# First sequences fetched by register, softmax by halves, first rows asked for per expert, in a fused two-layer mixture-of-experts and attention kernel

## Chip, cores and metric

The kernel runs on one core of a Trainium2 chip, in float32. A core has five engines that work side by side, each through its own queue in order: TensorE (PE, matrix products and transposes), VectorE (DVE), ScalarE (ACT), GpSimd (POOL) and SyncE (SP, which issues DMAs). ACT and POOL issue DMAs too. The metric is the device time of one execution in microseconds, as a median of several.

## Reference

Inputs are `x` (32 sequences of 64 rows of 256), gate probabilities of 32 sequences for 8 experts, a shared gate probability and a label `itok` per sequence, drawn from 0 to 2.

```
# first layer: dense mixture, then attention, added to x
c = (1 - sg) * sum_e prob[b,e] * (silu(x@Wg[e]) * (x@Wu[e])) @ Wd[e]  +  sg * shared(x)
q,k,v = c@W_qkv + b_qkv                       # 16 heads of 16
score = -arccosh(<q,k> on the hyperboloid)**2 / 4, causal
x = x + (softmax(score) * spike @ v) @ W_out + b_out

# second layer: an expert chosen by the label, two shared ones, weighed by a small gate
eo = relu(x@wi[label])@wo[label];  s0, s1 = relu(x@swi[i])@swo[i]
w  = softmax(relu([eo[:,0], s0[:,0], s1[:,0]] @ g1) @ g2)    # first row of each sequence
d  = eo*w0 + s0*w1 + s1*w2
d  = d + causal_attention(conv(layernorm(d)))                # rotary, softmax
d  = d + top1_moe(layernorm(d))                              # 4 experts
out = x + d
```

## The kernel before, in words

**Order of the sequences.** `order_of_sequences` (L127 to L220) reads the 32 labels twice, once as a row on every partition (`lab_row`) and once as a column (`lab_col`), both from ACT's queue, and sorts the sequences by label with small steps on DVE and three tiny matmuls: `row`, `col`, `same`, `lower`, ranks, `place`, and the one-hot `at` (L185). Two matmuls (L188, L189) turn `at` into row addresses of x (`tokens`, L193; as integers `tokens_i`, L196) and the sorted labels (`label`, L197). A constant block `setup`, also loaded by ACT, holds index tables used in these steps (at L158, L186, L193).

**Taking x in.** `gather` (L222 to L231) fetches 128 rows with an indirect DMA that POOL issues, at addresses from `tokens_i`. Rows come by blocks of 512 (eight sequences, four gathers). `take_in` (L558 to L569) transposes a block on PE (L565), copies it to `xT` (L566, two copies on DVE) and forms its sums `xS` (L537 to L541). The gathers of blocks 1 to 3 are asked for during the first expert.

**The dense mixture, L736 to about 1330 us.** Nine experts (the ninth is the shared one) over four blocks of 512 rows, each product cut into Strassen-like parts. `xg` (L777, POOL) is x weighed by the gate, `right` makes its sums `gS`, `left` (L492 to L500, DVE) the sums `wsum` of weights. `up` (L639) gives the up products: matmuls at L653, copies out of PSUM by ACT (L665), sums by DVE (L673), silu by ACT (L674). `down` (L599) is the down product. Weights come over SP, with one exception: the third of all, the first expert's Wd, goes out on POOL behind the first block's gathers (`issue_after(first_in)`). Beside the ninth expert's last blocks runs the first attention group, `hyperbolic(0)`.

**The middle, 1330 to 2110 us.** Eight groups of two tiles of 128 rows. A group passes through hyperbolic attention, `selected` (L883: two shared relu experts through `dense`, L899 and L913, then the chosen experts, L951 to L977; for some groups each half tile has its own weights, fetched at the label read into a register), `gated_sum` (L996), `rotary` and `route`. The steps of several groups are woven. For the first six groups, `selected` collects the first rows of all three outputs `eo[0..2]` in a tile `firsts` with six little DMAs (L993), and `gated_sum` transposes them at L1015.

**Attention.** `attend` (L335 to L387) works on scores `s` of 128 rows by 16 heads x 64 columns, `za` in the hyperbolic layer. Softmax is three whole steps: the maximum by heads (L339, DVE), the subtraction (L340, POOL), the exponential (L341, ACT). Then PE transposes in two lots of four (L348), copied out by DVE and ACT (L350, L352), and multiplies by the values `vb` (L359). Before it, scores are made at L307 (L264 to L296 prepare them) and masked at L331.

**The tail** is the mixture of four experts by blocks of sorted rows (L1408 to L1475).

**What sets the order.** Engines work their queues in order. A list scheduler fills the queues from the program's order, its own costs of instructions, and hints `issue_after(x)`, which keep an instruction behind x in that order. A tile in a pool with several buffers waits for its buffer's last readers. Completions of DMAs are counted on eight lanes; a DMA's issue waits until the DMA before it on the same lane is complete.

Of the kernel before, what the change touches and what calls it, by code (L numbers as in the profile page):

```python
# [10 lines left out]
F32 = mybir.dt.float32  # L11
I32 = mybir.dt.int32
AF = mybir.ActivationFunctionType
ALU = mybir.AluOpType
AX = mybir.AxisListType
PSUM = bass.MemoryType.PSUM

P = 128
B, S, D, H, HD, F = 32, 64, 256, 16, 16, 1024
NT = B * S // P  # L20
NE, NE2, NE3 = 8, 5, 4
FC = F // P
EPS = 1e-05
# [53 lines left out]
def adaln_attn_ffn_kernel(ctx: ExitStack, tc: tile.TileContext, a, consts, out):  # L77
    nc = tc.nc
    ctx.enter_context(nc.allow_non_contiguous_dma(reason="small per-channel vectors"))
    x_rows = a["x"].flatten_outer_dims()  # L80
    out_rows = out.flatten_outer_dims()

    const = ctx.enter_context(tc.tile_pool(name="const", bufs=1))


    ident = const.tile([P, P], F32, name="ident")
# [3 lines left out]
    tokens = const.tile([P, NT], F32, name="tokens")  # L90
    tokens_i = const.tile([P, NT], I32, name="tokens_i")
    label = const.tile([1, B], I32, name="label")
    causal = cst[:, C_CAUSAL : C_CAUSAL + S]
    headsel = cst[:, C_HEAD : C_HEAD + 4]
    cos = cst[:, C_COS : C_COS + HD]
# [7 lines left out]
    def rows(pool, name, n):  # L103

        t = pool.tile([P, n], F32, name=f"{name}_rows")
        nc.scalar.dma_start(t, a[name].partition_broadcast(P))
        return t

    def channels(name):

        t = const.tile([P, 2], F32, name=f"{name}_chan")
        nc.scalar.dma_start(t, a[name].rearrange("(c p) -> p c", p=P))
        return t
# [3 lines left out]
    def weight(pool, name, src, eng=None):  # L117

        t = pool.tile([P, src.shape[0] // P, src.shape[1]], F32, name=name)
        loaded.append((eng or nc.sync).dma_start(t, src.rearrange("(c p) n -> p c n", p=P)).ins)  # L120
        return t
# [5 lines left out]
    def order_of_sequences(pool, wide, psum, mixw):  # L127
# [4 lines left out]

        small = lambda name, n=1: pool.tile([B, n], F32, name=name)
        lab_row = pool.tile([B, B], I32, name="lab_row")
        nc.scalar.dma_start(lab_row, a["itok_B_0_2"].partition_broadcast(B))
        lab_col = pool.tile([B, 1], I32, name="lab_col")
        nc.scalar.dma_start(lab_col, a["itok_B_0_2"].unsqueeze(1))
        setup = pool.tile([P, C_COLS - C_SETUP], F32, name="setup")
        nc.scalar.dma_start(setup, consts[:, C_SETUP:])
        weights = small("weights", NE + 1)  # L140
# [6 lines left out]
        nc.gpsimd.memset(every, 1.0)  # L147

        row, col = small("row_f", B), small("col_f")
        nc.vector.tensor_scalar(col, lab_col, 0, NE2 - 1, ALU.max, ALU.min)  # L150
        nc.vector.tensor_scalar(row, lab_row, 0, NE2 - 1, ALU.max, ALU.min)
        same, lower = small("same", B), small("lower", B)
        nc.vector.tensor_scalar(same, row, col, None, ALU.is_equal)
        nc.vector.tensor_scalar(lower, row, col, None, ALU.is_gt)

# [29 lines left out]
        nc.vector.tensor_scalar(at, seq, place, None, ALU.is_equal)  # L185
        nc.vector.tensor_scalar(own, every, part, None, ALU.mult)  # L186
        pq = psum.tile([P, 512], F32, name="W1")
        nc.tensor.matmul(pq[:, 0:B], lhsT=own, rhs=at, start=True, stop=True)  # L188
        nc.tensor.matmul(pq[0:1, B : 2 * B], lhsT=col, rhs=at, start=True, stop=True)  # L189
        whose = pq[:, 0:B].rearrange("p (t k) -> p t k", k=2)  # L190
        for k in range(2):
# [1 line left out]
            nc.vector.tensor_scalar(  # L193
                tokens[half], whose[half, :, k], float(S), setup[half, C_POS : C_POS + 1], ALU.mult, ALU.add
            )
        ordered = nc.vector.tensor_copy(tokens_i, tokens).ins  # L196
        nc.vector.tensor_copy(label, pq[0:1, B : 2 * B])  # L197


        with tc.issue_after(ordered):  # L200
# [16 lines left out]
            stop=True,  # L217
# [107 lines left out]
    def heads(t):  # L325
        return t.rearrange("p (h j) -> p h j", j=S)
# [8 lines left out]
    def attend(s, vb, w_out, spike=None):  # L335


        mx = sb.tile([P, H], F32, name="mx", bufs=two)
        nc.vector.tensor_reduce(mx, heads(s), AX.X, ALU.max)  # L339
        nc.gpsimd.tensor_tensor(heads(s), heads(s), mx.unsqueeze(2).to_broadcast([P, H, S]), ALU.subtract)  # L340
        nc.scalar.activation(s, s, AF.Exp)  # L341
        yield
        sT = sb.tile([P, 8, P], F32, name="sT", bufs=two)
        for half in range(2):
            pt = turned()
            for i in range(4):
                hp = 4 * half + i
                nc.tensor.transpose(pt[:, i, :], s[:, hp * P : (hp + 1) * P], ident)  # L348
            if half:
                nc.scalar.copy(sT[:, 4 * half : 4 * half + 4, :], pt)  # L350
            else:
                nc.vector.tensor_copy(sT[:, 4 * half : 4 * half + 4, :], pt)  # L352
            yield
        py = bank([P, H, 17])
        for b2 in range(2):
            for hp in range(8):

                pair = hp % 4 // 2 * 4 + hp // 4 * 2 + hp % 2
                nc.tensor.matmul(  # L359
                    py[b2 * S : (b2 + 1) * S, 2 * pair : 2 * pair + 2, :],  # L360
                    lhsT=sT[:, hp, b2 * S : (b2 + 1) * S],
                    rhs=vb[:, b2, :, pair, :],
                    start=True,
                    stop=True,
                )
        inv = sb.tile([P, H], F32, name="inv", bufs=two)
        nc.vector.reciprocal(inv, py[:, :, 16])
        if spike is not None:
            nc.vector.tensor_scalar(inv, inv, spike, None, ALU.mult)
        y = sb.tile([P, D], F32, name="y", bufs=two)  # L370
        nc.vector.tensor_tensor(
            y.rearrange("p (h d) -> p h d", d=HD),
            py[:, :, 0:HD],
            inv.unsqueeze(2).to_broadcast([P, H, HD]),
            ALU.mult,
        )
        yield
        pt = turned()
        for c in range(2):
            nc.tensor.transpose(pt[:, c, :], y[:, c * P : (c + 1) * P], ident)  # L380
        yT = sb.tile([P, 2, P], F32, name="yT", bufs=two)
        nc.scalar.copy(yT, pt[:, 0:2, :])
        yield
        po = bank([P, D])
        for c in range(2):
            nc.tensor.matmul(po, lhsT=yT[:, c, :], rhs=w_out[:, c, :], start=c == 0, stop=c == 1)
        return po  # L387
# [114 lines left out]
    with ExitStack() as st:  # L502
# [13 lines left out]
        ordered = order_of_sequences(  # L516
            rp, lambda: work.tile([P, 2, TH], F32, name="cp", bufs=10).rearrange("p k n -> p (k n)"), psw, mixw
        )
        b_sur = rows(const, "L0_attn_b_sur", 1)
        threshold = rows(const, "L0_attn_threshold", 1)  # L520
        ln1_w, ln1_b = channels("L0_ffn_ln1_w"), channels("L0_ffn_ln1_b")
        ln2_w, ln2_b = channels("L0_ffn_ln2_w"), channels("L0_ffn_ln2_b")
        conv_w = const.tile([P, 2, 3], F32, name="conv_w")
        nc.scalar.dma_start(conv_w, a["L0_ffn_conv_w"].rearrange("(c p) o k -> p c (o k)", p=P))
        minus_b_sur = const.tile([P, 1], F32, name="minus_b_sur")
        with tc.issue_after(ordered):
            nc.vector.tensor_scalar(minus_b_sur, b_sur, -1.0, None, ALU.mult)
        eps = const.tile([P, 1], F32, name="eps")
        nc.vector.memset(eps, EPS)

        in_sums = None

        def right(eng, b, t):
# [19 lines left out]
        def gather_block(tb):  # L553
            for t in range(4 * tb, 4 * tb + 4, 2):
                got = gather(staged[t // 8][:, t % 8 : t % 8 + 2, :], t)
            return got
# [11 lines left out]
                )  # L568
            x_right.append(right(nc.vector if tb == 0 else nc.gpsimd, xT[tb], xS[tb]))  # L569

        first_in = gather_block(0)
        take_in(0)

        blank = rp.tile([P, ROW], F32, name="blank")
# [146 lines left out]
        for e in range(NE + 1):  # L721
            pick = lambda n, s: a[f"L0_cond_W{n}"][e] if e < NE else a[f"L0_cond_S{s}"]

            def take(left, src):
                nonlocal n_w
                i, j = n_w % 5, n_w % 4
                n_w += 1
                eng = nc.gpsimd if n_w == 3 else nc.sync
                with tc.issue_after(first_in) if n_w == 3 else nullcontext():
                    w = weight(rp if i in (2, 3) else wp, f"w{i}", src, eng)  # L730
                return left(w, (rp if j == 3 else wp).tile([P, 3, Q * P], F32, name=f"wsum{j}"))


# [5 lines left out]
            if e == 1:  # L739

                w_qkv = condp.tile([P, 2, 3 * D + 1], F32, name="w_qkv")
                nc.sync.dma_start(
                    w_qkv[:, :, 0 : 3 * D], a["L0_attn_W_qkv"].rearrange("(c p) n -> p c n", p=P)
                )
                nc.scalar.dma_start(
                    w_qkv[:, :, 3 * D], a["L0_attn_w_sur"].rearrange("(c p) -> p c", p=P)
                )
                b_qkv = rows(condp, "L0_attn_b_qkv", 3 * D)
            if e == 3:

                with tc.issue_after(loaded[-1]):
# [131 lines left out]
    def selected(g, xT):  # L883

        eo = [None] * 3
        output = lambda: rt.tile([P, NG, D], F32, name="eo", bufs=4)

        def dense(w):  # L890
# [32 lines left out]
        for s in range(2):  # L923
            po = yield from dense(slots(a["L0_cond2_swi"][s], a["L0_cond2_swo"][s]))
            eo[1 + s] = output()
            nc.vector.tensor_copy(eo[1 + s], po)

        def chosen(place):
            lab = nc.sync.value_load(label[0:1, place : place + 1], min_val=0, max_val=NE2 - 1)
# [56 lines left out]

        if g >= DIRECT:
            return eo, None

        firsts = hidden([P, 2, GN])[0 : 6 * NG, 0, :]  # L990
        for i in range(3):
            for b2 in range(2):
                nc.scalar.dma_start(firsts[4 * i + b2 : 4 * i + 4 : 2, :], eo[i][b2 * S : b2 * S + 1, :, :])  # L993
        return eo, firsts

    def gated_sum(g, eo, firsts):  # L996
# [567 lines left out]
```

## Time and profile before

| | us |
|---|---|
| median of 3 runs | 2293.69 |
| range of the runs | 2288.44 to 2294.05 |
| profiled execution | 2294.86 |
| its span | 2293.1 |
| mean granted TensorE clock | 0.993 |
| PE idle in the span | 72.1 |
| of it before 50 us | 17.5 |

The span is what the trace covers; the profiled execution's own time has 1.8 us around it. In a line of the page or of the list of groups, an operation has its line in the kernel (L665), engine, output and input tiles, count, busy time, mean duration and the idle time of its engine just before. In the list of waits, `PE X L653 <- ACT cp L665: 3.0, 3, 2.5` says that PE's matmuls into X at L653 stood idle for 3.0 us in 3 places, the longest 2.5, until ACT's copies at L665 ended. In the timeline a line is start, duration, engine, line and form, with the wait before it in brackets. In the table of stretches each row has its length, busy time and count of PE, PEld (weight load), DVE, ACT and POOL, then the granted clock, the DMA share and GB/s.

### The profile page before, as it was taken

The page shows a single profiled execution, that of the slowest core. Times are in us where ns is not written, and L with a number is a line of the kernel's source. Part 1 is how long each engine was busy: PE and PEld are TensorE (multiplying, and loading weights), DVE is VectorE, ACT ScalarE, POOL GpSimd, SP SyncE. Part 2 cuts the span into 40 slices and gives each one's busy share as a digit, 9 for nine tenths or more (in the row PEclk, how much of TensorE's full clock was granted, in tenths as well). Part 3 has the DMA queues.
Part 4 walks back from the last instruction along what each step waited for, and adds up shares of the span by engine and source line. Part 5 has one row for each costly group of instructions (what it writes and reads, how often), then busy time and mean ns, then how long its engine had stood idle before and what let it go on. Part 6 is the DMA issues. An engine that isn't in the chain of part 4 may idle for free. (4 is left out here: it accounts for less than half of the span.)

```text
span 2293.1 us, 29566 instructions
## 1 busy us (share of the span) xinstructions
PE 2221.0 (97%) x11222; PEld 1797.9 (78%) x11222; DVE 1323.4 (58%) x2443; ACT 741.1 (32%) x1184; POOL 799.5 (35%) x665
## 2 busy tenths in 40 slices
PE   6999999999999999999999999999999999989998
PEld 5888888888888888888888776677677677766665
DVE  7466575565655646556565744757757757554222
ACT  2333333333333333333333623424334334222111
POOL 6653444444444544445445350122122111111110
PEclk9999999999999999999999999999999999999999
DMA  3110010190101001001000046233332322540110
GB/s 118 35 37 19 1 38 19 56 309 1 37 19 37 19 1 37 19 18 38 1 19 10 3 142 200 83 121 106 97 94 83 93 87 80 189 136 24 40 38 24
DMA packets 100157, 145.02 MB, mean 63 GB/s; under 512 B 10214, under 2 KB 62000, under 8 KB 100016
## 3 DMA queue, kind: packets, MB, share of 16 engines
q1 hardware_dynamic: 81120, 124.45, 16.7%
q0 software_dynamic: 3952, 11.57, 1.5%
q10 hardware_dynamic: 14944, 7.11, 1.3%
q8 instruction: 90, 1.47, 0.3%
q14 instruction: 51, 0.42, 0.1%
HBM read 114.54 MB, written 24.29 MB: 61 GB/s over the span
## 5 line engine op out<-in xcount | busy, mean ns | idle before, releaser
L665 ACT COPY cp<-X 128x512 f32<-128x512 f32 x432 | 251.1, 585 | 537.2 <-PE X L653 523.7
L673 DVE TENSOR_TENSOR cp<-W,cp 128x512 f32<-128x512 f32 x272 | 186.2, 690 | 84.6 <-ACT cp L665 70.2
L706 POOL TENSOR_TENSOR h_t<-h_t,h_b 128x512 f32<-128x512 f32 x72 | 95.9, 1331 | 355.5 <-DVE h_t L675 355.4
L674 ACT ACTIVATE cp<-cp 128x512 f32<-128x512 f32 x216 | 136.4, 631 | 227.6 <-DVE cp L673 227.6
L777 POOL TENSOR_TENSOR xg<-xT,mixw 128x1024 f32<-128x1024 f32 x36 | 71.2, 1977 | 312.9 <-PE W L653 310.4
L899 PE MATMUL ph<-xT,slot 128*128 128x256 f32 x672 | 167.6, 391 | 1.6 <-ACT h L848 1.5
L913 PE MATMUL ph<-slot,h 128*128 128x256 f32 x672 | 165.1, 386 | 1.4 <-DVE h L850 0.9
L673 DVE TENSOR_TENSOR cp<-Y,cp 128x512 f32<-128x512 f32 x160 | 109.8, 689 | 89.5 <-PE Y L653 77.0
L675 DVE TENSOR_TENSOR h_b<-cp 128x512 f32<-128x512 f32 x144 | 141.3, 981 | 17.6 <-ACT cp L674 1.6
L653 PE MATMUL X<-xS,w 128*128 128x256 f32 x576 | 148.2, 380 | 2.7 <-ACT cp L665 2.7
L653 PE MATMUL X<-gS,w 128*128 128x256 f32 x576 | 148.3, 380 | 0.3 <-ACT cp L665 0.3
L899 PEld LDWEIGHTS ph<-xT,slot 128*128 128x128 f32 x672 | 124.3, 194 | 23.2 <-issue 6.6
L913 PEld LDWEIGHTS ph<-slot,h 128*128 128x128 f32 x672 | 121.8, 190 | 21.3 <-DVE h L850 5.0
L627 DVE TENSOR_TENSOR condT<-downA,condT 128x256 f32<-128x256 f32 x132 | 55.3, 419 | 142.4 <-PE downA L616 142.3
L616 PE MATMUL downA<-h_t,w 128*128 128x256 f32 x576 | 136.3, 379 | 0.0
L653 PEld LDWEIGHTS X<-xS,w 128*128 128x128 f32 x576 | 109.1, 190 | 18.1 <-ACT cp L665 3.8
L653 PEld LDWEIGHTS X<-gS,w 128*128 128x128 f32 x576 | 109.4, 190 | 16.0 <-ACT cp L665 0.7
L616 PEld LDWEIGHTS downA<-h_t,w 128*128 128x128 f32 x576 | 109.6, 190 | 14.7
L627 DVE TENSOR_TENSOR condT<-downB,condT 128x256 f32<-128x256 f32 x104 | 43.4, 417 | 122.9 <-PE downB L616 122.9
L709 POOL TENSOR_TENSOR h_t<-h_b,h_t 128x512 f32<-128x512 f32 x72 | 110.3, 1532 | 0.0
L707 POOL TENSOR_TENSOR h_t<-h_b,h_t 128x512 f32<-128x512 f32 x72 | 104.9, 1456 | 4.2
L708 POOL TENSOR_TENSOR h_t<-h_b,h_t 128x512 f32<-128x512 f32 x72 | 97.0, 1348 | 0.0
(366 smaller groups left out, 4565.1 us busy)
## 6 DMA issues: line engine op xcount, KB each, us to landing
rows_d<-blank SPq DMA_DIRECT2D x67, 258.0 KB
slot<-in_L_cond_swi SPq DMA_DIRECT2D x32, 512.0 KB
slot<-in_L_cond_swo SPq DMA_DIRECT2D x32, 512.0 KB
slot<-in_L_cond_wi SPq DMA_DIRECT2D x26, 512.0 KB
slot<-in_L_cond_wo SPq DMA_DIRECT2D x26, 512.0 KB
w<-in_L_cond_Wg SPq DMA_DIRECT2D x8, 1024.0 KB
w<-in_L_cond_Wu SPq DMA_DIRECT2D x8, 1024.0 KB
w_up<-in_L_ffn_expert_wv SPq DMA_DIRECT2D x16, 512.0 KB
```

The source lines that it names most:

```text
L616: nc.tensor.matmul(po, lhsT=wd[l](q), rhs=h[q // 2][r][:, q % 2, :], start=fresh and q == 0, stop=q == Q - 1, skip_group_check=True,)
L627: nc.vector.tensor_tensor(acc, po, acc, ALU.add)
L653: nc.tensor.matmul(bank[m, name][:, k, :], lhsT=w[l][:, q * P : (q + 1) * P], rhs=src[r], start=fresh and k == 0, stop=True, skip_group_ch ...
L665: nc.scalar.copy(side[m, name], bank[m, "X"])
L673: nc.vector.tensor_tensor(t, bank[m, b], t, ALU.add)
L674: nc.scalar.activation(side["g", name], side["g", name], AF.Silu)
L675: nc.vector.tensor_tensor(h[key], side["g", name], side["u", name], ALU.mult)
L707: nc.gpsimd.tensor_tensor(h["t2"], h["b22"], h["t1"], ALU.subtract)
L708: nc.gpsimd.tensor_tensor(h["t3"], h["b22"], b12, ALU.subtract)
L709: nc.gpsimd.tensor_tensor(h["t4"], h["b21"], h["t2"], ALU.subtract)
L899: nc.tensor.matmul(ph[:, k, :], lhsT=w[half][:, c, fc * P : (fc + 1) * P], rhs=xT[:, c, :], start=c == 0, stop=c == 1,)
L913: nc.tensor.matmul(po[:, k, :], lhsT=hs[fc // 2][:, fc % 2, k * P : (k + 1) * P], rhs=w[2 + fc // 4][:, fc % 4, :], start=fc == 0, stop=fc ...
```

## The change

It has three parts.

1. `lab_col` is gone; `lab_row` goes out on SP; `col` is made from `row` by a product with the identity and a sum. A third small matmul makes `seqs`, the numbers of the first eight sequences in sorted order. SP and ACT read them into registers, four each, and fetch one sequence of 64 rows each at a register address, in place of block 0's four gathers on POOL. A number of small loads on ACT (b_sur to conv_w) and, on SP, the first Wd and w_qkv stand behind these; Wd goes over SP as the other weights do. `minus_b_sur` moves to POOL in the second expert.
2. In `attend`, maximum, subtraction and exponential are done on halves of 512 columns, eight heads each.
3. `firsts` is allotted at the start of `selected`, and the two DMAs of an expert are asked for right behind that expert's output.

```diff
-        nc.scalar.dma_start(lab_row, a["itok_B_0_2"].partition_broadcast(B))
-        lab_col = pool.tile([B, 1], I32, name="lab_col")
-        nc.scalar.dma_start(lab_col, a["itok_B_0_2"].unsqueeze(1))
+        nc.sync.dma_start(lab_row, a["itok_B_0_2"].partition_broadcast(B))
...
         row, col = small("row_f", B), small("col_f")
-        nc.vector.tensor_scalar(col, lab_col, 0, NE2 - 1, ALU.max, ALU.min)
         nc.vector.tensor_scalar(row, lab_row, 0, NE2 - 1, ALU.max, ALU.min)
         same, lower = small("same", B), small("lower", B)
+        nc.vector.tensor_tensor(lower, row, ident[0:B, 0:B], ALU.mult)
+        nc.vector.tensor_reduce(col, lower, AX.X, ALU.add)
...
         pq = psum.tile([P, 512], F32, name="W1")
+        nc.tensor.matmul(pq[0:1, 2 * B : 2 * B + 8], lhsT=part, rhs=at[:, 0:8], start=True, stop=True)
+        first_eight = nc.vector.tensor_copy(seqs, pq[0:1, 2 * B : 2 * B + 8]).ins
...
-        ordered = nc.vector.tensor_copy(tokens_i, tokens).ins
-        nc.vector.tensor_copy(label, pq[0:1, B : 2 * B])
+        with tc.issue_after(first_eight):
+            ordered = nc.vector.tensor_copy(tokens_i, tokens).ins
+            nc.vector.tensor_copy(label, pq[0:1, B : 2 * B])
...
-        nc.vector.tensor_reduce(mx, heads(s), AX.X, ALU.max)
-        nc.gpsimd.tensor_tensor(heads(s), heads(s), mx.unsqueeze(2).to_broadcast([P, H, S]), ALU.subtract)
-        nc.scalar.activation(s, s, AF.Exp)
+        for half in range(2):
+            of = slice(half * 512, (half + 1) * 512)
+            mh = mx[:, half * 8 : half * 8 + 8]
+            nc.vector.tensor_reduce(mh, heads(s[:, of]), AX.X, ALU.max)
+            nc.gpsimd.tensor_tensor(heads(s[:, of]), heads(s[:, of]), mh.unsqueeze(2).to_broadcast([P, 8, S]), ALU.subtract)
+            nc.scalar.activation(s[:, of], s[:, of], AF.Exp)
...
-        first_in = gather_block(0)
+        behind_x = [None, None]
+        for place in range(8):
+            eng = (nc.sync, nc.scalar)[place % 2]
+            seq = eng.value_load(seqs[0:1, place : place + 1], min_val=0, max_val=B - 1)
+            half = place % 2 * S
+            got = eng.dma_start(staged[0][half : half + S, place // 2, :], x_rows[bass.ds(seq * S, S), :])
+            behind_x[place % 2] = got.ins
+        with tc.issue_after(behind_x[1]):
+            b_sur = rows(const, "L0_attn_b_sur", 1)
+            threshold = rows(const, "L0_attn_threshold", 1)
...
-                eng = nc.gpsimd if n_w == 3 else nc.sync
-                with tc.issue_after(first_in) if n_w == 3 else nullcontext():
-                    w = weight(rp if i in (2, 3) else wp, f"w{i}", src, eng)
+                with tc.issue_after(behind_x[0]) if n_w == 3 else nullcontext():
+                    w = weight(rp if i in (2, 3) else wp, f"w{i}", src)
...
+                with tc.issue_after(behind_x[0]), tc.issue_after(behind_x[1]):
+                    nc.sync.dma_start(
+                        w_qkv[:, :, 0 : 3 * D], a["L0_attn_W_qkv"].rearrange("(c p) n -> p c n", p=P)
+                    )
+                    nc.scalar.dma_start(
+                        w_qkv[:, :, 3 * D], a["L0_attn_w_sur"].rearrange("(c p) -> p c", p=P)
+                    )
+                    b_qkv = rows(condp, "L0_attn_b_qkv", 3 * D)
...
+        firsts = hidden([P, 2, GN])[0 : 6 * NG, 0, :] if g < DIRECT else None
+
+        def gather_first(i):
+            for b2 in range(2 if g < DIRECT else 0):
+                nc.scalar.dma_start(firsts[4 * i + b2 : 4 * i + 4 : 2, :], eo[i][b2 * S : b2 * S + 1, :, :])
...
             nc.vector.tensor_copy(eo[1 + s], po)
+            gather_first(1 + s)
...
-        firsts = hidden([P, 2, GN])[0 : 6 * NG, 0, :]
-        for i in range(3):
-            for b2 in range(2):
-                nc.scalar.dma_start(firsts[4 * i + b2 : 4 * i + 4 : 2, :], eo[i][b2 * S : b2 * S + 1, :, :])
+        gather_first(0)
         return eo, firsts
```

More of the change, by code (lines that the diff above doesn't have):

```diff
@@ L92, in adaln_attn_ffn_kernel @@
     label = const.tile([1, B], I32, name="label")
+    seqs = const.tile([1, 8], I32, name="seqs")
     causal = cst[:, C_CAUSAL : C_CAUSAL + S]
@@ L518, in adaln_attn_ffn_kernel @@
         )
[L519 to L529, printed above, removed]
         in_sums = None
@@ L569, in take_in @@
             x_right.append(right(nc.vector if tb == 0 else nc.gpsimd, xT[tb], xS[tb]))
-        first_in = gather_block(0)
+        behind_x = [None, None]
[8 more added lines that the diff above has]
+            threshold = rows(const, "L0_attn_threshold", 1)
+            ln1_w, ln1_b = channels("L0_ffn_ln1_w"), channels("L0_ffn_ln1_b")
+            ln2_w, ln2_b = channels("L0_ffn_ln2_w"), channels("L0_ffn_ln2_b")
+            conv_w = const.tile([P, 2, 3], F32, name="conv_w")
+            nc.scalar.dma_start(conv_w, a["L0_ffn_conv_w"].rearrange("(c p) o k -> p c (o k)", p=P))
+            eps = const.tile([P, 1], F32, name="eps")
+            nc.vector.memset(eps, EPS)
         take_in(0)
@@ L741, in adaln_attn_ffn_kernel @@
                 w_qkv = condp.tile([P, 2, 3 * D + 1], F32, name="w_qkv")
[L742 to L748, printed above, removed]
+                with tc.issue_after(behind_x[0]), tc.issue_after(behind_x[1]):
[6 more added lines that the diff above has]
+                    b_qkv = rows(condp, "L0_attn_b_qkv", 3 * D)
+                minus_b_sur = const.tile([P, 1], F32, name="minus_b_sur")
+                with tc.issue_after(in_sums):
+                    nc.gpsimd.tensor_scalar(minus_b_sur, b_sur, -1.0, None, ALU.mult)
             if e == 3:
```

## The prediction

> **What bounds the kernel now.** I read the totals of the page first, then the busy time by stretches, then TensorE's list of waits, then the timeline of the front and of one softmax, and last how the instructions are ordered after the change.
>
> ```profile
> PE 2221.0 (97%) x11222; PEld 1797.9 (78%) x11222; DVE 1323.4 (58%) x2443; ACT 741.1 (32%) x1184; POOL 799.5 (35%) x665
> ```
>
> TensorE (PE) is busy 2221.0 of 2293.1 us, and the granted clock is 0.993. The change leaves its matmuls as they are (one tiny one is added), so at most the 72.1 us of idle can be won. By stretches (busy us of each engine):
>
> ```profile
> 0.00:10.00 10.00, 0.37 (x4) 0.28 (x4) 3.25 (x23) 0.00 (x0) 1.32 (x9) 1.00 0.75 232
> 10.00:20.00 10.00, 3.94 (x11) 1.93 (x11) 6.17 (x19) 1.28 (x1) 6.21 (x5) 1.00 0.56 165
> 50.00:1200.00 1150.00, 1150.00 (x5337) 1014.31 (x5337) 678.08 (x955) 373.22 (x634) 547.23 (x437) 1.00 0.11 38
> 1400.00:2100.00 700.00, 662.69 (x4118) 488.64 (x4117) 438.12 (x1085) 238.94 (x357) 124.75 (x104) 0.98 0.35 109
> ```
>
> From 50 to 1200 there is no idle to win. 15.7 us lie before 20 us (10 − 0.37 and 10 − 3.94), 37.3 us between 1400 and 2100. The change acts in these two places. The waits of PE by operand and releaser (us, times, longest):
>
> ```profile
> PE W L172 <- DVE kind L169: 8.5, 1, 8.5
> PE ph L1015 <- DMA vb<-v: 5.5, 3, 1.9
> PE pt L348 <- ACT s L341: 5.2, 8, 1.4
> PE ph L1015 <- DMA h<-eo: 4.7, 3, 1.8
> PE X L565 <- DMA w<-in_x,tokens_i: 3.1, 4, 1.6
> PE X L653 <- ACT cp L665: 3.0, 3, 2.5
> PE pt L348 <- ACT za L341: 0.8, 2, 0.5
> ```
>
> The first and fifth are the front, the third and last the softmax (6.0 together), the second and fourth the first rows (10.2 together). Idle on DVE, ACT or POOL counts only where it ends one of these.
>
> **Part 1: the first eight sequences, fetched by register.** The front's chain, in the timeline (start, duration, in brackets the wait):
>
> ```profile
> 4.05 0.17 DVE L151 TENSOR_SCALAR row_f<-lab_row 32x32 f32<-32x32 int32 x1 [3.18 <-DMA lab_row<-in_itok_B]
> 6.17 0.14 DVE L150 TENSOR_SCALAR col_f<-lab_col 32x1 f32<-32x1 int32 x1 [1.95 <-DMA lab_col<-in_itok_B]
> 10.76 0.63 PE L188 MATMUL W<-at,cp 32*128 32x32 f32 x2 [1.91 <-DVE at L185]
> 12.80 1.41 POOL L225 DMA_INDIRECT w<-in_x,tokens_i  x1 [10.88 <-DVE minus_b_sur L527]
> 20.65 0.90 PE L565 MATMUL X<-ident,w 128*128 128x128 f32 x3 [0.66 <-DMA w<-in_x,tokens_i]
> 21.59 0.69 DVE L566 COPY xT<-X 128x512 f32<-128x512 f32 x1 [1.71 <-PE X L565]
> 22.38 2.26 POOL L777 TENSOR_TENSOR xg<-xT,mixw 128x1024 f32<-128x1024 f32 x1 [2.46 <-DVE xT L566]
> ```
>
> lab_col lands 2.1 us after lab_row. It goes; col is made from row by two small DVE steps (0.17 to 0.23 each by their neighbours), so `same` starts at about 4.85 instead of 6.34. L186, which needs setup, now stands in front (0.27). Setup goes out on ACT at 0.75 and lands at 4.1 as lab_row did, or at 5.7 if it takes the 4.9 of lab_col. `at` ends at 9.3 instead of 10.70: 1.4 won, bounds 0 to 1.8.
>
> The new matmul (0.3) and the copy to `seqs` (0.17) end at 9.85. The label loads of before began their second step 0.6 after `label` was ready, and run 0.59 apart; with a third register step (0.15) and the transfer's issue (0.33) I take 0.9 to the first fetch and 1.15 between fetches on a queue. SP and ACT take four each: 10.75, 11.9, 13.05, 14.2. The gathers landed 2.6 to 3.7 us after issue, lab_row 3.3; I take 3.0. Places 0 to 3 are in at 14.9, 4 to 7 at 17.2, where before the last transposes began at 20.65. On POOL four gathers go (5.2 us of issue), with Wd's issue behind them at 18.94.
>
> What is late next is DVE. The first X copy (about 16.2) has three steps of the second weight sum (0.67 each) behind it, then the second X copy at about 18.95; xg on POOL starts at 19.7 instead of 22.38. This is 2.7 won, although the rows come 3.4 earlier. The later stall of 0.70 at 31.65 (PE behind an ACT copy) should go too, since DVE, ACT and POOL are all ahead: 3.4. Against it: the gathers for block 1 stay on POOL and now end last, landing about 32.7 where PE comes for them at about 32.9; up to 0.7 is lost if they slip.
>
> Queues passed: SP carries four value loads and fetches ahead of Wd, and waits for `seqs` meanwhile; behind them are Wd, w_qkv and the 13 label loads, of which only Wd is wanted early. Issued at 15 it lands at 21.1 (6.2 by its row of before), well ahead of the first down product. ACT carries the same ahead of b_sur, threshold and the rest; its first copy is wanted at about 20.6, and w_sur's issue, which waits for Wd on the same completion lane, stands between its first and second copies (21.1 against about 23). The cover is 1 to 2 us; without it the slip goes straight to PE. So the front gives **−3.2** (3.4 less a little for that), bounds −5 to −1.
>
> [...]
>
> The first four-matmul groups of L653 took 1.92 us, later ones 1.03. [...]
>
> **Part 2: softmax by halves.** One step of 128 x 1024 is 1.21 on DVE (L339), 1.90 on POOL (L340), 1.06 on ACT (L341), 4.2 in line before L348 may begin. Half-size rows near them: DVE reduce of 480 columns 0.65, POOL L404 1.04, ACT L674 0.63. The first half is ready after 2.3, the second after 3.4 (POOL sets the pace). The first half's four transposes (0.27 each) cover most of the 1.1 between. There are 32 such steps; halving adds 0.1 on DVE, 0.18 on POOL and 0.20 on ACT to each, on engines busy 35 to 63% here, so it costs nothing if nobody waits for the sum. I take half of the 6.0 us of L348 as won: **−3.0**. It can't be all, since the list is of what came last, and behind `s` PE next waits for sT (1.2 at L359) or scores. Bounds: −6, and +4 if the reordered middle gaps elsewhere.
>
> One further place: in the first hyperbolic step, woven into the ninth expert, ACT stands behind POOL's 2.88 at L340 and PE waits behind ACT:
>
> ```profile
> 1311.14 1.06 ACT L341 ACTIVATE za<-za 128x1024 f32<-128x1024 f32 x1 [2.29 <-POOL za L340]
> 1312.72 1.13 PE L653 MATMUL X<-xS,w 128*128 128x256 f32 x4 [2.46 <-ACT cp L665]
> ```
>
> The halves let one exponential pass earlier, but the second still stands ahead of the copies: **−0.4**.
>
> **Part 3: first rows asked for at once.** In the trace of before, four of a group's six little transfers (L993) already go before the chosen expert's copy is made, by the scheduler's choice:
>
> ```profile
> 1425.09 3.10 ACTq L993 DMA_DIRECT2D h<-eo  x4
> 1428.60 0.37 ACT L984 COPY eo<-ph 128x256 f32<-128x256 f32 x1 [3.00 <-PE ph L977]
> 1429.00 1.17 ACTq L993 DMA_DIRECT2D h<-eo  x2
> 1434.03 0.26 PE L1015 MATMUL ph<-ident,h 12*128 12x12 f32 x2 [1.87 <-DMA vb<-v]
> ```
>
> The last two follow the chosen expert's copy in both kernels, and L1015 waits for them: the 10.2 stays, **0**. The tile `firsts` holds one of nine hidden buffers longer; PE waits 2.6 in all for h at L899 and L913, so that is small.
>
> **Sum.** −3.2 − 3.0 − 0.4 + 0 = −6.6 against the profiled execution's 2294.86 (span 2293.1 and 1.8 around it), which gives 2288.3. That execution lies 1.17 above the median of 2293.69, so as a median I forecast 2287.1. A difference of 0.3% (6.9 us) is about what a measurement of this kernel can tell from no change.
>
> **Rivals.**
> *The gain is taken by the next limiter.* DVE's weight sums, the block-1 gathers or w_sur's wait on ACT eat half of the front, and L348's stalls go over to sT. The front then gives 1.9 and the rest nothing: 2291.8. For it: the DVE binding above. Against: 2.7 of the front is left after counting that.
> *The first rows do come earlier,* so that part 3 does what it says: with four transfers off ACT's queue at the end, all of the 10.2 goes too: 2276.9. For it: L1015 waits in six groups. Against: the rows above.
> *Slower: more waits on ACT's queue.* ACT works in order, and an exponential that waits for POOL holds all that stands behind it. At L341 ACT waits 25.5 us in 17 waits now (16.9 in 13 and 8.6 in 4), 1.5 each. With halves there are twice as many exponentials; 17 more waits of up to 1.04 (POOL's half) are 17.7, and if they reach PE through copies and relus behind them, 17.7 − 6.6 gives 2304.8. It decides above 0.39 us a wait (6.6/17). For it: the 2.46 above. Against: ACT is 34% busy from 1400 to 2100, and PE waits little for ACT elsewhere there.
>
> **Chances.** Forecast 0.60 (2280 to 2296 by itself; 0.36 of it beyond 6.9, 0.22 within, 0.02 slower), next limiter 0.12, first rows 0.10, ACT's queue 0.18. Faster by over 0.3%: 0.36 + 0.10 = 0.46. Slower: 0.18 + 0.02 + 0.01 = 0.21. The rest, 0.33, is the same. The range 2279 to 2299 leaves out most of the third and of the fourth case, about 0.19.
>
> **What would show it.** Right: xg of the first block starts at 19 to 20.4, the last L565 of block 0 at 17 to 18.5; L348's waits sum to about 3; L1015's stay near 10; POOL has no gather before 24. Wrong: xg after 21.5, a new wait at L653 before 50 us on ACT or on block 1's gathers, L1015's waits gone, or PE waits on ACT beyond 10 us more in 1400 to 2100.

## The result and the profile after

The changed kernel takes 2282.51 us in the median of ten runs (2279.50 to 2284.43), the kernel before 2290.06 beside it in ten (2285.08 to 2294.05). The ratio is 0.9963, 95% interval 0.9954 to 0.9972: about 8.5 us less (the two medians lie 7.6 apart; below, a part's worth in us is its ratio's distance from 1 times 2291 us unless the text says otherwise). The forecast was 2287.1 and 6.6 less; 3.6 of the distance in absolute time is the median of the kernel before, which three runs had put at 2293.69. The profiled execution of the changed kernel took 2280.21, its span is 2278.4.

The totals of the page after, and the busy time by stretches (length, busy us and count of PE, PEld, DVE, ACT, POOL, then granted clock, DMA share, GB/s):

```profile
PE 2213.1 (97%) x11224; PEld 1795.4 (79%) x11224; DVE 1327.2 (58%) x2476; ACT 746.0 (33%) x1216; POOL 800.4 (35%) x693
```

```profile
0.00:10.00 10.00, 1.39 (x10) 0.94 (x10) 5.22 (x34) 0.00 (x0) 1.32 (x9) 1.00 0.64 229
10.00:20.00 10.00, 7.42 (x18) 4.42 (x18) 8.11 (x14) 1.87 (x2) 1.45 (x1) 1.00 0.51 148
50.00:1200.00 1150.00, 1150.00 (x5338) 1015.41 (x5337) 675.29 (x950) 372.65 (x633) 545.45 (x433) 1.00 0.11 38
1400.00:2100.00 700.00, 664.91 (x4128) 489.58 (x4127) 443.43 (x1117) 244.90 (x388) 129.72 (x132) 0.99 0.34 109
```

The span is 14.7 shorter between these two executions, more than between the medians: a profile is one execution, and that of the kernel before (2294.86) lies above all ten of its runs here. PE's idle fell from 72.1 to 65.3, and 4.5 of that lies before 20 us (15.7 to 11.2). But PE's *busy* time also fell, by 7.9, with two matmuls more. Work that is the same and takes less time points to the clock. The clock record of the trace shows TensorE at half clock for 27.3 us between 1300 and 2100 in the kernel before and for 10.2 in the changed one; half of the difference is 8.5. (The record begins only with the first full clock, at 25.4 and 19.7 us. The 1.00 in the rows ahead of that is no measurement: four matmuls of a product take 1.9 us there and 1.03 later.)

PE's waits after (the lines have moved: L653 is L663, L565 is L559, L348 is L354, L359 is L365, L1015 is L1032, L264 is L267):

```profile
PE ph L1032 <- DMA h<-eo: 5.5, 4, 1.5
PE W L172 <- DVE kind L169: 5.4, 1, 5.4
PE at L267 <- DVE hc L1133: 4.7, 8, 0.9
PE X L559 <- DMA w<-in_x: 2.7, 1, 2.7
PE at L365 <- ACT sT L356: 2.6, 3, 1.1
PE ph L1032 <- DMA vb<-v: 2.5, 2, 1.3
PE X L663 <- ACT cp L675: 2.4, 2, 2.2
PE pt L354 <- ACT za L347: 2.0, 3, 0.8
PE pt L354 <- ACT s L347: 1.6, 6, 0.4
```

The front's two waits fell from 8.5 to 5.4 and from 3.1 to 2.7, the softmax's for ACT from 6.0 to 3.6 (another 0.9 at L354 is now put down to DVE), the first rows' from 10.2 to 8.0. In return L365 and L267 rose. Their rows before were:

```profile
PE at L264 <- DVE hc L1116: 3.6, 7, 0.9
PE at L359 <- ACT sT L350: 1.2, 1, 1.2
```

Not all of this is the work of the part that acts there. With the front alone changed, the first rows' waits are 8.4 and L267's 4.5 already. The front's chain in the timeline after:

```profile
2.48 0.17 DVE L149 TENSOR_SCALAR row_f<-lab_row 32x32 f32<-32x32 int32 x1 [1.61 <-DMA lab_row<-in_itok_B]
7.41 0.23 DVE L185 TENSOR_SCALAR at<-setup,place 32x32 f32<-32x32 f32 x1
9.07 4.44 ACTq L571 DMA_DIRECT2D w<-in_x  x4
11.70 0.45 PE L559 MATMUL X<-ident,w 128*128 128x128 f32 x1 [2.74 <-DMA w<-in_x]
16.88 0.85 PE L559 MATMUL X<-ident,w 128*128 128x128 f32 x3
17.77 0.69 DVE L560 COPY xT<-X 128x512 f32<-128x512 f32 x1 [0.88 <-PE X L559]
18.55 2.27 POOL L790 TENSOR_TENSOR xg<-xT,mixw 128x1024 f32<-128x1024 f32 x1 [16.62 <-DVE xT L560]
```

The labels are there at 2.48 instead of 4.05, `at` starts 3.06 earlier, xg 3.83, and PE comes to the transposes of block 1 at 32.05 instead of 36.21 (these are matmuls; the expectations below name the weight loads, 0.2 earlier).

### The profile page after: what moved, and what is told of

Read it like the earlier page. It is cut to its first block, busy times and chain, and to the rows that moved or that the text cites. A ratio compares the mean times of both kernels' runs of the same rounds, so it can differ in the third digit from the quotient of the medians.

```text
span 2278.4 us, 29746 instructions
## 1 busy us (share of the span) xinstructions
PE 2213.1 (97%) x11224; PEld 1795.4 (79%) x11224; DVE 1327.2 (58%) x2476; ACT 746.0 (33%) x1216; POOL 800.4 (35%) x693
## 5 line engine op out<-in xcount | busy, mean ns | idle before, releaser
L919 PE MATMUL ph<-xT,slot 128*128 128x256 f32 x672 | 166.1, 389 | 1.5 <-ACT h L861 1.5
L663 PE MATMUL X<-xS,w 128*128 128x256 f32 x576 | 148.4, 380 | 2.4 <-ACT cp L675 2.4
L663 PE MATMUL X<-gS,w 128*128 128x256 f32 x576 | 148.2, 380 | 0.0
L919 PEld LDWEIGHTS ph<-xT,slot 128*128 128x128 f32 x672 | 123.1, 192 | 23.3 <-issue 7.1
L663 PEld LDWEIGHTS X<-xS,w 128*128 128x128 f32 x576 | 109.2, 191 | 18.2 <-ACT cp L675 4.1
L663 PEld LDWEIGHTS X<-gS,w 128*128 128x128 f32 x576 | 109.5, 190 | 15.2 <-issue 0.6
```

Source lines behind the costliest of these rows:

```text
L663: nc.tensor.matmul(bank[m, name][:, k, :], lhsT=w[l][:, q * P : (q + 1) * P], rhs=src[r], start=fresh and k == 0, stop=True, skip_group_ch ...
L919: nc.tensor.matmul(ph[:, k, :], lhsT=w[half][:, c, fc * P : (fc + 1) * P], rhs=xT[:, c, :], start=c == 0, stop=c == 1,)
```

## The experiments

Ratios are to the kernel before, run beside each; "clock" is the mean granted clock over a kernel's runs (0.9942 over the 56 runs of the kernel before, 0.9955 for the changed one). "By place" means by the moment at which PE reaches the same instruction in two profiles.

### Each part alone

The edits are the hunks of the diff, cut by part.

```diff
# front_only: all hunks but those in attend, selected
# halves_only
+        for half in range(2):
...
+            nc.scalar.activation(s[:, of], s[:, of], AF.Exp)
# firsts_only
+        firsts = hidden([P, 2, GN])[0 : 6 * NG, 0, :] if g < DIRECT else None
...
+            gather_first(1 + s)
```

**The front alone.**

> Part 1 alone: order of the sequences, fetch by register and the queues behind it; softmax and first rows as before. Theory (the front gives most): PE reaches the transposes of block 1 at about 31.8 us as in the changed kernel (36.00 before), the later stages keep their waits (L348 about 6, L1015 about 10), so -4.3 us, ratio about 0.9981. Rival (the front's gain is given back by the reordered steps behind it, and what the median shows comes from the middle): block 1 early all the same, but PE's idle behind 50 us grows by about as much; ratio 0.9995 to 1.0005.

Measured: 0.9969 (0.9957 to 0.9981), clock 0.9942. L348's waits (5.4 + 0.8) and L1015's (8.4) stay about as they were, as the theory said. Its ratio of 0.9981 is the interval's end, and its place was missed: block 1's transposes start at 33.42, 2.8 us earlier than before and not 4.2 (why, is told further down). So the ratio gives 7.1 us, of which 2.8 are seen by place in this profile. The rival's ratio falls.

**The halves alone.**

> Part 2 alone: softmax by halves. Theory: L348's waits fall from 6.0 to about 3.5, ACT's waits for POOL at the exponential rise from 25.5 to about 45 us without reaching PE, so -2 to -3.5 us, ratio 0.9985 to 0.9992. Rival (ACT's queue): the 20 us more of ACT waits hold copies and relus back, PE's waits on ACT from 1400 to 2100 grow by more than 3, ratio 1.000 or above.

Measured: 1.0018 (1.0007 to 1.0029), slower by 4 us, clock 0.9928. The rows of PE's list of waits (L348 is L351, L359 is L362):

```profile
PE at L264 <- DVE hc L1119: 4.6, 8, 0.9
PE at L362 <- ACT sT L353: 3.0, 3, 1.5
PE pt L351 <- ACT za L344: 2.4, 5, 0.8
PE pt L351 <- ACT s L344: 1.6, 6, 0.4
PE pt L351 <- DVE goes L1332: 0.9, 1, 0.9
```

The wait at L348 for ACT fell to 4.0, as expected, and ACT's waits for POOL at the exponential rose from 25.5 to 44.0. But PE's idle in the span is 72.4 (2291.7 − 2219.3), before 72.1: L362 rose by 1.8, the 0.9 on DVE is new, and L264 rose by 1.0. Neither theory had that. PE's waits on ACT from 1330 to 2110 are 12.3 in sum, before 12.2, so ACT's queue is not the cause. Nor are waits the cause of the 4 us, as far as this profile shows: it is 1.4 us shorter than that of the kernel before. The runs point to the clock: 0.9928 against 0.9945 beside it, and 0.0017 of 2291 us is 3.9 (an estimate).

**The first rows alone.**

> Part 3 alone: the first rows asked for behind each expert's output. Theory: the two transfers behind the chosen expert's copy still end the wait at L1015, 10.2 us stays within 2; 0 +- 1.5 us, ratio 0.9994 to 1.0006. Rival (ACT's queue is shorter at the end of a group, so the last two land earlier): L1015's waits fall to 8 or less and the ratio goes to 0.9985.

Measured: 1.0050 (1.0037 to 1.0064), slower by 11.5 us, clock 0.9912. L1015's waits are 10.5, as the theory said, and yet its ratio failed; the rival's failed too. The page of this kernel shows why its account by waits is too small:

```profile
PE 2228.6 (97%) x11222; PEld 1799.1 (78%) x11222; DVE 1325.6 (57%) x2443; ACT 741.4 (32%) x1184; POOL 801.3 (35%) x665
```

The same 11222 matmuls as before are busy for 7.6 us longer, and the idle is 77.1, 5.0 more. By stretches of 4 us, right behind one of the waits for the first rows (at 1530.72):

```profile
1528.00:1532.00 4.00, 2.00 (x12) 0.90 (x11) 1.53 (x3) 0.00 (x0) 1.04 (x1) 1.00 0.47 149
1532.00:1536.00 4.00, 3.54 (x20) 2.18 (x20) 2.64 (x9) 0.89 (x3) 0.00 (x0) 0.54 0.12 26
1536.00:1540.00 4.00, 4.00 (x17) 3.44 (x16) 0.38 (x3) 1.88 (x3) 0.00 (x0) 0.61 0.05 11
```

PE is half idle for 4 us, and for 6.8 us after it the granted clock is 0.5. This profile has eight such falls between 1300 and 2100, three of them right behind a wait for the first rows; the profile of the kernel before has four there, that of the changed kernel two. (This profile is the slowest of the kernel's five runs.)

### Do the parts add?

The order of instructions on each engine falls into a front (before 50 us) and a middle, and neither part of the change touches the other's: in front_only the middle stands exactly as before. The part on the first rows reorders PE's matmuls too, not only the transfers. Parts 2 and 3 together make another middle than either alone.

```diff
# halves_firsts = hunks in attend + hunks in selected
# front_halves  = front hunks + hunks in attend
```

> Parts 2 and 3 together, the front as before. From 1200 us on the order of instructions is that of the changed kernel, before 50 us that of the kernel before. Theory (the order in the middle decides, and the two parts make another order together than each alone): the front's worth comes off, so the ratio is that of the whole change over that of the front, 0.9963/0.9969 = 0.9994, +-0.001; the granted clock stays at about 0.9945. Rival (the parts add): 1.0018 x 1.0050 = 1.0068, granted clock 0.990 or less.

Measured: 0.9999 (0.9988 to 1.0009), clock 0.9950. The parts do not add; the theory's value is inside.

> Parts 1 and 2 together, the first rows as before. Theory (front and middle add, since neither changes the other's order): 0.9969 x 1.0018 = 0.9987, +-0.001, so that part 3 on top of it is worth -5 us although alone it cost 12.6. Rival (where TensorE's clock drops in the middle hangs on the moment at which it starts, so the front's shift of 4 us moves the drops): ratio between 0.996 and 0.9975, near the whole change, with a granted clock of 0.995 or more instead of 0.9928.

Measured: 0.9983 (0.9974 to 0.9992), clock 0.9942. Front and middle add (0.9987 expected); the rival's range is missed.

So the ratios stand in a table of front and middle:

| middle | front before | front after |
|---|---|---|
| as before | 1 | 0.9969 |
| halves | 1.0018 | 0.9983 |
| first rows | 1.0050 | not run |
| both | 0.9999 | 0.9963 |

The front is worth 7 to 8 us with each of the three middles. The halves cost 3 to 4 (4 with a lower mean clock than the kernel beside it, but 3 on top of the front with the same one, 0.9942; so the clock doesn't settle it). The first rows cost 11.5 alone, and are worth 4.5 on top of the halves (1.0018 to 0.9999, and 0.9983 to 0.9963). Both together are worth nothing that these intervals can tell.

### Inside the front

```diff
# labels_beside_wg, on the changed kernel
-        nc.sync.dma_start(lab_row, a["itok_B_0_2"].partition_broadcast(B))
+        nc.scalar.dma_start(lab_row, a["itok_B_0_2"].partition_broadcast(B))
```

> The changed kernel with one line back: the labels are loaded from ACT's queue again, as its first DMA, while SP starts with Wg (1 MB) at the same moment; in the changed kernel the labels go first on SP and Wg follows. Theory A (a transfer started beside Wg shares the DMA engines with it): the labels take 3.2 us again, row_f starts at about 4.0 instead of 2.48 and block 1's transposes are 1.5 later, 33.3. Theory B (it was the queue or the second label load, not Wg): row_f stays at 2.5 and nothing moves.

The timeline of that run:

```profile
0.75 0.46 SPq L121 DMA_DIRECT2D w<-in_L_cond_Wg  x1
4.04 0.17 DVE L149 TENSOR_SCALAR row_f<-lab_row 32x32 f32<-32x32 int32 x1 [3.17 <-DMA lab_row<-in_itok_B]
6.93 0.27 DVE L186 TENSOR_SCALAR cp<-cp,setup 32x128 f32<-32x128 f32 x1 [2.72 <-DMA setup<-consts]
11.60 0.23 DVE L185 TENSOR_SCALAR at<-setup,place 32x32 f32<-32x32 f32 x1
```

Theory A's time holds for the labels (4.04; by what means Wg delays them this run doesn't show), but not its 1.5 us: setup, issued at 1.24, is there only 5.7 later, where in the changed kernel L186 runs at 2.75. `at` starts at 11.60, 4.2 later than in the changed kernel and 1.1 later than before, and xg at 22.70, 4.2 later than in the changed kernel and 0.3 later than before. Block 1's transposes start at 37.60; 1.4 of that is a fall of the clock that this profile has and the changed kernel's hasn't (one group of four matmuls takes 1.91 there instead of 1.03). So the one line, by which a load of 4 KB goes ahead of Wg, is the front's whole gain by place. ACT's queue as such is not slow: in the changed kernel setup goes out on it at 0.75, with Wg 0.47 behind on SP, and is used 2.0 later. (One run, 2287.28.)

```diff
# labels_first, on the kernel before
-        nc.scalar.dma_start(lab_row, a["itok_B_0_2"].partition_broadcast(B))
-        lab_col = pool.tile([B, 1], I32, name="lab_col")
-        nc.scalar.dma_start(lab_col, a["itok_B_0_2"].unsqueeze(1))
+        nc.sync.dma_start(lab_row, a["itok_B_0_2"].partition_broadcast(B))
... (col from row, as in the change)
```

> The kernel before with the labels loaded once, first on SP ahead of Wg, and the column made from the row; the gathers stay on POOL and all else as before. Theory (the labels' place ahead of Wg is the front's gain, 3.3 of its 4.2): the one-hot `at` ends at about 7.6 instead of 10.70, xg of block 0 starts at about 19.1, block 1's transposes at about 32.8 instead of 36.00, ratio 0.998 to 0.9986. Rival (the fetch by register gives most): xg stays above 21 because the gathers on POOL or the weight sums hold it, block 1's transposes above 34.5.

```profile
9.75 1.41 POOL L224 DMA_INDIRECT w<-in_x,tokens_i  x1 [7.82 <-DVE minus_b_sur L526]
19.32 2.27 POOL L776 TENSOR_TENSOR xg<-xT,mixw 128x1024 f32<-128x1024 f32 x1 [2.45 <-DVE xT L565]
```

Block 1's transposes start at 33.17. With POOL's gathers kept, 3.0 of the 4.2 us are there; the fetch by register gives about 1. In the time the theory's 3 us do not show: 0.9996 (0.9987 to 1.0005), 0.9 us, clock 0.9935. The kernel beside it has 0.9940, and 0.0005 of 2291 us is 1.1 (an estimate): about half of what is missing. So the gain by place is shown for this line alone, but its worth in time is not.

### Two steps further

```diff
# xg_halves, on the changed kernel: the first block's xg in two operations of 256 rows
+                cuts = 2 if e == 0 and tb == 0 else 1
+                for cut in range(cuts):
...
# after_warm, on the changed kernel, in gated_sum of the last two groups
+                nc.tensor.transpose(room[:, P * (1 + i % 3) : P * (2 + i % 3)], eo[0][:, NG - 1, 0:P], ident)
... (twice ahead of gh, three times ahead of pl; room is the unused rest of their bank)
```

> The changed kernel with the first block's xg (L790) made in two halves of 256 rows, the first as soon as the first half of xT is copied (14.96), so that POOL ends at about 19.7 instead of 20.82. Theory (TensorE's 1.7 us wait before xg at 21 is POOL's start): block 1's transposes at about 30.6 instead of 31.84, the rest as in the changed kernel, -1.2 us on it, ratio to the kernel before 0.9950 to 0.9963. Rival: the wait goes to xS on VectorE (0.94 to 2.12 a step beside POOL), block 1's transposes stay at 31.5 or later.

Measured: 0.9958 (0.9945 to 0.9971). PE starts the products of xg at 18.92 without a wait, but block 1's transposes start at 31.27, 0.8 earlier and not 1.2. PE then waits 0.95 for xS on DVE at 22.20, where the changed kernel waits 1.71 for it at 21.15: the rival's wait at about half the size. The place lies between the two theories, and the ratio inside the theory's range.

> The changed kernel with five extra transposes into an unused corner of PSUM in the last two groups, put where TensorE waits for small steps of the gate (ahead of L1048 and L1062), so that it has fewer gaps there; they leave the result as it is. In the changed kernel the granted clock falls to half for about 6 us at 1956 and again at 2028, right behind these gaps. Theory (gaps of TensorE, however short each, bring the clock down when they come close together): the fall at 1956 to 1964 goes, 2 to 3 us less at that place, granted clock 0.997; the one at 2028 stays, since a 3.7 us wait for nT comes with it. Rival (the clock falls at random, or by the kind of matmul): the falls stay, and the extra work costs 1 us.

Measured: 0.9955 (0.9940 to 0.9969), clock 0.9960 (0.997 was expected). The place in question, first of the changed kernel, then of this one:

```profile
1952.00:1956.00 4.00, 3.22 (x30) 2.12 (x27) 0.92 (x4) 0.96 (x3) 0.00 (x0) 1.00 1.01 333
1956.00:1960.00 4.00, 3.19 (x16) 2.81 (x17) 1.77 (x7) 1.48 (x2) 0.00 (x0) 0.81 1.04 391
1960.00:1964.00 4.00, 4.00 (x16) 3.32 (x15) 2.93 (x10) 0.60 (x1) 0.00 (x0) 0.76 0.64 236
```

```profile
1952.00:1956.00 4.00, 3.65 (x34) 2.54 (x31) 0.93 (x4) 0.96 (x3) 0.00 (x0) 1.00 0.98 343
1956.00:1960.00 4.00, 4.00 (x27) 3.58 (x26) 1.76 (x7) 2.00 (x3) 0.00 (x0) 1.00 1.03 387
1960.00:1964.00 4.00, 4.00 (x20) 3.54 (x19) 3.35 (x11) 1.13 (x3) 0.00 (x0) 1.00 0.98 308
```

In the changed kernel PE has gaps of 0.46 and 0.78 us right ahead of the fall, which here lasts 3.4 us and not the 6 of the expectation. The edit fills them, and not with idle transposes alone: the scheduler also moved four matmuls of the next step (L919) into the second gap. First the changed kernel, then this one:

```profile
1956.03 0.61 PE L1048 MATMUL ph<-fold,h 128*128 128x4 f32 x4 [0.46 <-ACT h L1044]
1957.42 1.05 PE L1062 MATMUL ph<-g,h 128*128 128x3 f32 x8 [0.78 <-DVE h L1051]
```

```profile
1956.64 1.03 PE L919 MATMUL ph<-xT,slot 128*128 128x256 f32 x4
```

With the gaps filled the clock stays at 1.00. This is more than one profile's luck: each of the ten profiles without the extra transposes has a fall that begins between 1955 and 1985, and neither of the two with them has. The transposes of the first tail block start at 2027.17 instead of 2029.49, 2.3 earlier, although both kernels stand at 1870.3 at the last first rows. The fall at 2028, where PE waits 3.7 for nT, stayed, and it lasts 10.2 us instead of 6.8. At the first place it came as the theory had it (granted clock 1.00 where it was 0.81 and 0.76); in the ratio the 2 to 3 us are within the interval's width.

> The same extra transposes on top of the kernel with xg in halves, the fastest so far. Theory: 0.8 us from the front and 2 to 3 from the clock, ratio 0.9940 to 0.9955. Rival (no worth in either): 0.9963.

Measured: 2278.26 us, 0.9943 (0.9930 to 0.9957), clock 0.9965. This is the lowest median of all kernels run here, some 4 us under the changed kernel's, and inside the theory's range: block 1 starts at 31.27, the first tail block at 2026.11 (32.05 and 2029.49 in the changed kernel).

## Why the prediction was right, and where it was not

**The sign and the size** were right: 6.6 less was forecast, 8.5 measured. But the way to the number was half right, and that the sum came out is in good part luck: of its terms only the front's gave time by itself.

**Front, −3.2 forecast.** By place PE gained 4.2 at block 1 in the changed kernel (2.8 in front_only's profile). The term that was mis-sized is the arrival of labels and setup. I took 3.3 and some 3.4 us for them, by the row of lab_row in the kernel before; alone ahead of Wg the labels took 1.7 (issued 0.75, used at 2.48). That row was measured with Wg issued at the same moment (0.74, and 0.75 for the labels); in the changed kernel Wg goes out at 1.22, 0.47 behind the labels. From `at` on the terms held roughly: 0.9 to the first fetch was 1.0, 1.15 between fetches was 1.31 (ACT's four start at 9.07, 10.46, 11.75 and 13.01), landing 3.0 was 2.6 to the first use. The 0.70 at 31.65 that I added to the front was the wait of the weight load (PEld); PE's own wait there was 0.29:

```profile
31.65 1.13 PE L653 MATMUL X<-gS,w 128*128 128x256 f32 x4 [0.29 <-ACT cp L665]
```

What came late next was not DVE, as I had it: the second xT copy waited 0.88 for PE, whose second lot of transposes stood behind the first products (16.88). The cover of 1 to 2 us for w_sur on ACT held, and block 1's gathers did not end last.

The front also has matmuls that run slow, for which the forecast has no term. Before, the first groups of four at L653 took 1.92 and the later ones 1.03. The instructions of front_only's front are those of the changed kernel, but in its profile the products of xg ran so:

```profile
21.74 1.91 PE L660 MATMUL X<-xg,w 128*128 128x256 f32 x4
23.45 1.79 PE L660 MATMUL Y<-xg,w 128*128 128x256 f32 x4
```

against 1.03 each in the changed kernel; block 1 began at 33.42 instead of 32.05. In the traces both start the last products of this step ahead of xg at 17.5, but the first full clock is recorded at 18.16 in front_only and at 19.71 in the changed kernel, and only front_only falls back, for 3.4 us from 21.57. Why only one of the two does is not shown.

The front's worth by ratios, 7 to 8 us, is more than its 4.2 by place (the ratios' intervals reach down to 4.4 for front_only). Where the rest lies stays open: the order behind the front is the same, no wait explains it, and neither does the clock, at least for front_only (0.9942, and 0.9945 for the kernel beside it).

**Softmax, −3.0 forecast.** The wait fell as worked out, and its worth was not there. L348's waits for ACT fell by 2.4, and ACT's by-product was as worked out (from 25.5 to 45.1 at the exponential, 19.6 where I had 17.7):

```profile
  POOL s L346: 37.1, 17
  POOL za L346: 8.0, 13
```

It didn't reach PE, so the rival on ACT's queue fell. But the step "half of the 6.0 as won" failed: in halves_only most of what L348 gave went to sT at L362, as the rival on the next limiter had it, and to a wait of 0.9 for DVE (hc at L264 rose too, but it did so with the front alone). By PE's idle the term is +0.3 in halves_only against the kernel before, and −2.0 in front_halves against front_only (65.5 and 67.5); by the ratios it is +3 to +4 us. That is the size of the bound "+4 if the reordered middle gaps elsewhere", but not its cause, since the idle didn't grow by that; what cost it stays open, with the lower clock of halves_only as the only sign.

**The place at 1312, −0.4 forecast.** 2.46 became 2.17:

```profile
1307.93 1.13 PE L663 MATMUL X<-xS,w 128*128 128x256 f32 x4 [2.17 <-ACT cp L675]
```

**First rows, 0 forecast.** The last two transfers still follow the chosen expert's copy and end the wait, as said:

```profile
1424.82 0.37 ACT L1005 COPY eo<-ph 128x256 f32<-128x256 f32 x1 [3.06 <-PE ph L998]
1425.22 1.17 ACTq L906 DMA_DIRECT2D h<-eo  x2
1429.74 0.26 PE L1032 MATMUL ph<-ident,h 12*128 12x12 f32 x2 [1.35 <-DMA vb<-v]
```

Of the 10.2 us 8.0 stayed, and 8.4 with the front alone; the rival that the first rows come earlier, so that all of it goes, fell. But 0 as the worth of the part was wrong in both directions: +11.5 alone, −4.5 behind the halves.

**The sum** treated the parts as independent. They are not: 0.9969 x 1.0018 x 1.0050 is 1.0037, and 0.9963 was measured. That −3.0 and 0 for the middle lay near the −0.2 to −1.4 of both together (0.9999; 0.9963 against 0.9969) came from errors that cancel: luck, in plain words. What I left out as a term behind the front is the clock. In the kernel before it falls to half behind the first rows' wait of 1.87 at 1434:

```profile
1432.00:1436.00 4.00, 2.13 (x15) 1.25 (x16) 1.53 (x5) 0.00 (x0) 1.04 (x1) 0.89 0.58 152
1436.00:1440.00 4.00, 3.53 (x19) 2.23 (x12) 2.01 (x6) 1.21 (x2) 0.00 (x0) 0.50 0.41 126
1440.00:1444.00 4.00, 4.00 (x19) 3.43 (x18) 0.82 (x5) 2.40 (x4) 0.00 (x0) 0.76 0.00 1
```

In the four profiles with both parts in the middle and nothing else there, where this wait is 1.7 us at most, it never falls there; in the six with one of them or none, where it is up to 2.0, it falls behind one to three of the six waits in all but one. A longer wait alone doesn't decide: falls follow waits of 1.74 to 2.00, and other waits of 1.74 to 1.89 have none behind them. In the clock records of the kernel before and of the changed one, the stretches between two changes last 3.41, 6.83, 10.24, 17.07, 68.27 us and longer, all multiples of 3.41. Counted off from those changes in pieces of 3.41 us, the wait of 1.87 at 1434 lies whole in the last piece ahead of the fall:

```profile
1431.71:1435.12 3.41, 1.54 (x8) 0.88 (x6) 1.34 (x3) 0.00 (x0) 1.04 (x1) 1.00 0.61 173
1435.12:1438.53 3.41, 2.94 (x18) 1.32 (x16) 1.80 (x6) 0.37 (x1) 0.00 (x0) 0.50 0.52 158
```

The other wait of 1.87 in that profile, at 1617, lies across two pieces with 0.66 and 1.20 us of idle, and no fall is behind it. At the ten remaining waits of these two profiles PE was idle for 1.58 or less of any one piece, and half clock follows none of them. This is what two executions show, with a single fall behind a wait among them; how much idle brings the clock down they don't show. That the shorter waits keep the clock up is the likely reason for the 4.5 us that the first rows give behind the halves; it fits the profiles, but each is one execution, and no run varied that wait by itself.

## What to carry to other kernels

Where one engine is busy for 97% of the time, an edit that moves waits between its neighbours is worth what it does to that engine's idle and to its clock, not the wait that it removes; read both from the page, busy time at the same count of matmuls included. Parts of a change that pass through a list scheduler must be run in combination, since two losses alone can be no loss together. And the small loads that start the critical chain go ahead of the first large one (the labels were used at 2.48 so, and at 4.04 beside it); here this is shown by place, not yet in time.

## What the hardware showed that was not expected

From issue to use, a 4 KB load of labels issued at the same moment as a 1 MB load on another queue took 3.3 us, and 1.7 when it went 0.47 ahead of it; setup took 5.7 when it was issued at 1.24, half a microsecond behind the large load, and 2.0 or less when it went first on its queue (0.75 to 2.75).

The runs of halves_only differ mostly by the clock: the eleven go from 2290.82 us at a mean clock of 0.995 to 2301.20 at 0.991, 10.4 us for 0.004. Between 1300 and 2100 the falls last 6.8, 3.4, 10.2 and 6.8 us at half clock in the kernel before, 3.4 and 6.8 in the changed one and 10.2 in the two with extra transposes. The one of 3.4 at 1958.5 costs 1.7: the 28 matmuls at 1958.34 take 7.98 us in the changed kernel and 6.29 in after_warm, where the clock stays up. In the 3.4 us ahead of it (1955.1 to 1958.5, where most of PE's work is small matmuls of 4 and 3 columns) stand two gaps of 0.46 and 0.78 us, and PE is idle for 1.25 us in all. At 1523.9 to 1527.3 in the kernel before it is idle for 1.58 us, and half clock does not follow, so idle time alone does not account for these falls. Filling the gaps with transposes and moved matmuls took the fall away (granted clock 1.00 from 1956 to 1964 in after_warm).
